# A graph network on one core: a shorter last edge batch, zeros for the padding rows from a tile of their own, and the last count store on another queue

## The chip, the core and the metric

The kernel runs on one core of a Trainium2 chip. The core has TensorE for matrix products (PE in the profile, PEld for its weight loads), VectorE (DVE), ScalarE (ACT), GpSimd (POOL) and SyncE (SP). Here SP does nothing but issue DMAs. ScalarE issues some too: a DMA that stands in ScalarE's order is issued when its turn comes, between its other instructions. TensorE writes its results to PSUM, and VectorE and ScalarE carry them from there to SBUF.

The metric is the device time of one execution in microseconds (us). The kernel before took 1538.35 us, the median of 3 runs from 1538.09 to 1540.38. The profile comes from one further execution.

## The reference, cut to what matters

There are 3125 nodes with 128 features and 103125 edges, sorted by their destination: 50000 random pairs in both directions and one loop per node. Four graph layers follow each other, each added to its input and normalised. The first multiplies by a weight matrix and sums over the edges with a weight per edge; the second is graph attention with four heads, the third attention between neighbours, the fourth two rounds of averaging over neighbours.

```python
# layer 0
xw = x @ weight
out = relu(segment_sum(edge_val[:, None] * xw[edge_col], edge_row) + b)
x = layernorm(x + out)
# layers 1 to 3 need for each pair (destination, source) only how many edges join them
```

## The kernel before, in words

The kernel turns the edge list into two dense matrices over 25 x 25 blocks of 128 nodes (`NB` = 25, so 3200 rows and columns for 3125 nodes; the last 75 are padding). One, `wd`, holds for each pair of nodes the sum of the edge weights in f32. The other, `f_ctd`, holds the count of edges in bf16, transposed. Both go to HBM. Layer 0 multiplies with `wd`; the layers after it read `f_ctd`.

**The start (lines 558 to 753).** The edges are loaded, keys are computed and stored as the table `td`, and five indirect DMAs on GpSimd (line 646) gather the edges of 128 groups of nodes each. `keys_of` turns one gather into keys in bf16 (copies on ScalarE and VectorE, lines 532, 534, 667, 687, 691, transposes on TensorE). ScalarE's queue carries the small loads: weights, biases, `f_att` (lines 538, 700, 711). The rows of `x` come over SP; the last 53 of them are a DMA of their own (line 642), after which SP issues nothing until the first store of the loop.

**The edge loop (lines 811 to 901).** A group is 5 nodes (`WN`), a batch 16 groups (`BW`), so there are 40 batches of 80 nodes (`NBT` = 40), the last for nodes 3120 to 3199. For each batch, `make` has VectorE compare the keys with a ramp to get one-hot matrices: `ohd` and `ohc` (line 824, two instructions of 128 x 4096) and `wod`, `ohd` scaled by three parts of the weight (line 833, three instructions). ScalarE scales 16 more columns of 128 for the third part (line 842, in `more`, four at a time). `make(b + 1)` is called before batch `b` is multiplied, so VectorE works one batch ahead. TensorE then does four groups of four windows: 8 matmuls into `cp` (counts, line 864) and 24 into `wp` (weights, line 872). ScalarE copies `cp` into `cs` (line 877) and `wp` into `ws` (line 883). After each batch SP stores `ws` to `wd` in two DMAs (line 885: 112 and 13 partitions, runs of 512 B), and after every second batch `cs` to `f_ctd` (line 888: 3200 runs of 320 B).

As soon as a block row of `wd` (128 nodes) is stored, `add0` loads it in two halves, `cw` (line 790, three buffers of 640 KB), and multiplies it with `xw` for 20 of the 25 column blocks (line 794). Block row 23 needs batches up to 38, block row 24 needs batches 38 and 39. The last block rows are done after the loop (line 900). Then come `bias0` for the five other column blocks (line 782), the normalisation of layer 0 (`end0`, line 799), and a second pass over `wd` for those five blocks (line 1162).

**What sets the order.** The program is written in the tile framework: a scheduler puts every engine's instructions in one order and adds the waits, and each engine and each queue keeps that order. The DMAs of SP's and ScalarE's queues get eight completion semaphores in turn, in the order of the program; a DMA is issued only when the last user of its semaphore has landed. Buffers come from pools; a tile waits until the work on the buffer's last tile is over.

Of the kernel before, what the change touches and what calls it, by code (L numbers as in the profile page):

```python
# [7 lines left out]
F32 = mybir.dt.float32  # L8
# [3 lines left out]
OP = mybir.AluOpType  # L12
# [3 lines left out]
P = 128  # L16
N = 3125
NB = 25
NP = NB * P
# [470 lines left out]
WN = 5  # L490
NW = 640
NG = 5
BW = 16
KW = WN * NB
NBT = NW // BW
Z0 = 20
V1 = 100
GA = 80.0
# [7 lines left out]
def fast_path(  # L506
# [4 lines left out]
    nc = tc.nc  # L511
# [3 lines left out]
    ctd = dram.tile([NB, P, NP], BF16, name="f_ctd")  # L515
    wd = dram.tile([NP, NP], F32, name="wd")
# [49 lines left out]
    ep = front.enter_context(tc.tile_pool(name="f_ep", bufs=1))  # L566
    cps = front.enter_context(tc.tile_pool(name="f_cps", bufs=3, space=PSUM))
    ramp = ep.tile([P, P], BF16, name="ramp")
# [156 lines left out]
    def products_of_weights():  # L725
        nc.gpsimd.tensor_tensor(both, gb_row, sb_row, OP.add)
        tw = {}
        for name, w in (("l1", l1_wt), ("q", wqt), ("k", wkt), ("v", wvt)):
            t = zps.tile([P, P], F32, name="trw", tag="acc3")
            nc.tensor.transpose(t, w, ident)  # L730
            tw[name] = ep.tile([P, P], F32, name="tw_" + name)
            nc.scalar.copy(tw[name], t)
        t = zps.tile([P, P], F32, name="trw", tag="acc3")
        nc.tensor.matmul(t[:, 0 : 2 * H], tw["l1"], att, start=True, stop=True)
        nc.scalar.copy(watt, t[:, 0 : 2 * H])
        t = zps.tile([P, P], F32, name="trw", tag="acc3")
        nc.tensor.matmul(t, tw["q"], tw["k"], start=True, stop=True)
        nc.scalar.copy(wyv[:, 0:P], t)
        t = zps.tile([P, P], F32, name="trw", tag="acc3")
        nc.tensor.matmul(t, tw["v"], wot, start=True, stop=True)  # L740
        nc.scalar.copy(wyv[:, P:], t)

    def xw_of(b0, n):

        t = zps.tile([P, 512], F32, name="trx", tag="acc0")
        for k in range(n):
            nc.tensor.transpose(t[:, k * P : (k + 1) * P], x[:, b0 + k, :], ident)
        xT = ep.tile([P, 512], F32, name="f_xTb", bufs=2)
        nc.scalar.copy(xT[:, : n * P], t[:, : n * P])
        t = zps.tile([P, 512], F32, name="trx", tag="acc2")  # L750
        for k in range(n):
            nc.tensor.matmul(t[:, k * P : (k + 1) * P], xT[:, k * P : (k + 1) * P], l0_wt, start=True, stop=True)
        nc.scalar.copy(xw[:, b0 : b0 + n, :].rearrange("p b d -> p (b d)"), t[:, : n * P])
# [26 lines left out]
    def bias0(acc, n):  # L780
        for j in range(n):
            nc.tensor.matmul(acc[:, j, :], ones, l0_br, start=(j == 0), stop=False, skip_group_check=True)
# [16 lines left out]
    def end0(acc, b0, n):  # L799
        t = lp0.tile([P, 4, P], F32, name="r0")  # L800
        nc.vector.scalar_tensor_tensor(
            t[:, 0:n, :], acc[:, 0:n, :], 0.0, x[:, b0 : b0 + n, :], OP.max, OP.add
        )
        layer_norm(lp0, x[:, b0 : b0 + n, :], t, (0, n), True)
# [3 lines left out]
    SB = 2  # L808
    wv_ = wd.rearrange("(w i) (c d) -> w (i c) d", i=WN, d=P)

    def make(b):

        if b % 8 == 2 and 8 < b < NBT - 8:
            keys[b // 8 + 1] = keys_of(b // 8 + 1)
        kd2, kc2, w2, w3 = keys[b // 8]
        ohd = op_.tile([P, 2 * BW, P], BF16, name="ohd")
        ohc = op_.tile([P, 2 * BW, P], BF16, name="ohc")

        def twos(k):
            k = k[:, b % 8, :, :, :].rearrange("p q w t -> p (q w) t")  # L820
            return k[:, :, None, :].to_broadcast([P, 2 * BW, P // 2, 2])

        for o, k in ((ohd, kd2), (ohc, kc2)):
            nc.vector.tensor_tensor(
                o.rearrange("p w (a t) -> p w a t", t=2), twos(k),
                ramp.rearrange("p (a t) -> p a t", t=2)[:, None, :, :].to_broadcast([P, 2 * BW, P // 2, 2]),
                OP.is_equal,
            )
        wod = []
        for s in range(3):  # L830
            f = of_.tile([P, 2 * BW, P], BF16, name="wod")
            n = 2 * BW if s < 2 else BW
            nc.vector.tensor_tensor(  # L833
                f[:, 0:n].rearrange("p w (a t) -> p w a t", t=2), ohd[:, 0:n].rearrange("p w (a t) -> p w a t", t=2),
                twos(w2[s])[:, 0:n], OP.mult,
            )
            wod.append(f)

        def more(k):
            for w in range(k, k + 4):  # L840
                at = (b % 8) * BW + w
                nc.scalar.activation(wod[2][:, BW + w, :], ohd[:, BW + w, :], AF.Copy, scale=w3[:, 1, at : at + 1])  # L842

        return ohd, ohc, wod, more

    cs = None
    acc0 = None
    done = 0
    cur = make(0)
    for k in range(0, BW, 4):  # L850
        cur[3](k)
    for b in range(NBT):
        ohd, ohc, wod, _ = cur
        cur = make(b + 1) if b + 1 < NBT else None
        if b % SB == 0:
            cs = sp.tile([P, NB, SB * BW * WN], BF16, name="cs")
        ws = sp.tile([P, BW, P], F32, name="ws")
        for k in range(0, BW, 4):
            cp = cps.tile([P, 4, P], F32, name="cp", tag="cw")
            wp = cps.tile([P, 4, P], F32, name="wp", tag="cw")  # L860
            for j in range(4):
                for q in range(2):
                    w = q * BW + k + j
                    nc.tensor.matmul(  # L864
                        cp[:, j, 0:KW], ohd[:, w, :], ohc[:, w, 0:KW], start=(j == 0 and q == 0), stop=(j == 3 and q == 1),
                        skip_group_check=True,
                    )
            for j in range(4):
                for q in range(2):
                    w = q * BW + k + j  # L870
                    for s in range(3):
                        nc.tensor.matmul(  # L872
                            wp[:, j, :], ohc[:, w, :], wod[s][:, w, :], start=(j == 0 and q == 0 and s == 0),
                            stop=(j == 3 and q == 1 and s == 2), skip_group_check=True,
                        )
            i0 = (b % SB) * BW * WN + k * WN
            nc.scalar.copy(  # L877
                cs[:, :, i0 : i0 + 4 * WN].rearrange("p c (w i) -> p c w i", i=WN),
                cp[:, :, 0:KW].rearrange("p w (i c) -> p c w i", c=NB),
            )  # L880
            if cur:
                cur[3](k)
            nc.scalar.copy(ws[:, k : k + 4, :], wp)  # L883
        for a, e in ((0, 112), (112, KW)):
            nc.sync.dma_start(wv_[b * BW : (b + 1) * BW, a:e, :].rearrange("w k d -> k w d"), ws[a:e, :, :])
        if b % SB == SB - 1:
            i0 = (b - SB + 1) * BW * WN
            nc.sync.dma_start(ctd[:, :, i0 : i0 + SB * BW * WN].rearrange("c d i -> d c i"), cs)
        if b < 2:
            for blocks in GB[4 * b : 4 * b + 4]:  # L890
                xw_of(*blocks)
        if b == 2:
            products_of_weights()
            acc0 = [zps.tile([P, 4, P], F32, name=f"acc{k}", tag=f"acc{k}") for k in range(Z0 // 4)]
            for a in acc0:
                bias0(a, 4)
        while acc0 and (done + 1) * P <= (b - 1) * BW * WN:
            add0(zp, done, acc0, (0, Z0))
            done += 1
    for i in range(done, NB):  # L900
        add0(zp, i, acc0, (0, Z0))
    front.close()
# [147 lines left out]
    with ExitStack() as st:  # L1050
# [20 lines left out]
        zpp = zero.enter_context(tc.tile_pool(name="f_zpp", bufs=1, space=PSUM))  # L1071
        left = GB[Z0 // 4 :]
        acc1 = [zpp.tile([P, 4, P], F32, name=f"left{k}") for k in range(len(left))]
        t8 = zpp.tile([P, 512], F32, name="tr_sa")
        for a, (b0, n) in zip(acc1, left):
            bias0(a, n)
        for g in range(Z0 // 4):
            end0(acc0[g], *GB[g])
# [73 lines left out]
        def top():  # L1152
            heads(0, Z0)
            ex = fp.tile([P, H], F32, name="ex", bufs=1)
# [135 lines left out]
        for x_, (g, hp, c) in enumerate(items):  # L1290
            i0, n = IG[g]
# [42 lines left out]
    with ExitStack() as st:  # L1334
# [79 lines left out]
        for x_, (q, c) in enumerate(items):  # L1414
            i0, n = QG[q]
# [5 lines left out]
            if q == 0 and NB - 4 <= c < NB - 1:  # L1421
                a = split + (c - NB + 4) * 512
# [6 lines left out]
            elif c == NB - 1:  # L1429
# [5 lines left out]
                for k0 in range(0, n, 3):  # L1435
                    m = min(3, n - k0)
                    t = acc[k0 // 3][:, 0 : m * (P + 1)].rearrange("p (b d) -> p b d", d=P + 1)
# [3 lines left out]
                    for j in range(m):  # L1441
                        b = i0 + k0 + j
# [9 lines left out]
    with ExitStack() as st:  # L1452
# [8 lines left out]
        for g in range(3, len(GB)):  # L1461
            b0, n = GB[g]
# [18 lines left out]
        for b in range(NB - HB):  # L1481
# [5 lines left out]
            if b == 18:  # L1487
# [3 lines left out]
                t = ps.tile([P, 512], F32, name="tr")  # L1491
# [37 lines left out]
        for k in range(K + 3):  # L1529
            if k < K:  # L1530
                for b in range(NB - HB, NB):
                    add1(last[b], b, k)
                c, n = CH[k]
# [86 lines left out]
```

## Time and profile before

| | before |
|---|---|
| median of 3 runs | 1538.35 us |
| the profiled execution | 1536.56 us |
| its span | 1534.5 us |
| TensorE busy | 1400.5 us (91%) |
| VectorE, ScalarE busy | 981.0, 923.4 us |
| mean granted TensorE clock | 0.979 |
| first one-hot matrix starts (line 824) | 31.45 us |
| last matmul of the edge loop starts a run of 1.50 us (line 872) | 467.27 us |
| matmuls of block rows 23 and 24 (line 794) | 487.28 to 497.87 us |
| DMA packets, bytes | 210368, 224.39 MB |

Times in the profile count from the start of the span. In the timeline a row is a run of equal instructions: start, duration, engine, line, operation, output and inputs, number; in brackets how long the engine was idle before it and what ended that. SPq and ACTq are DMA issues on the two queues; their duration is the time from the first issue of the row to the end of the last, waits within the row included. In the windows a row is a stretch of time, with the busy time of each engine (and its instructions), the granted TensorE clock as a share, the mean busy share of the 16 DMA engines, and what they moved in GB/s. The durations are those of one execution.

### The profile page before, as it was taken

The page shows a single profiled execution, that of the slowest core. Times are in us where ns is not written, and L with a number is a line of the kernel's source. Part 1 is how long each engine was busy: PE and PEld are TensorE (multiplying, and loading weights), DVE is VectorE, ACT ScalarE, POOL GpSimd, SP SyncE. Part 2 cuts the span into 40 slices and gives each one's busy share as a digit, 9 for nine tenths or more (in the row PEclk, how much of TensorE's full clock was granted, in tenths as well). Part 3 has the DMA queues.
Part 4 walks back from the last instruction along what each step waited for, and adds up shares of the span by engine and source line. Part 5 has one row for each costly group of instructions (what it writes and reads, how often), then busy time and mean ns, then how long its engine had stood idle before and what let it go on. Part 6 is the DMA issues. An engine that isn't in the chain of part 4 may idle for free.

```text
span 1534.5 us, 35155 instructions
## 1 busy us (share of the span) xinstructions
PE 1400.5 (91%) x14871; PEld 1223.6 (80%) x14871; DVE 981.0 (64%) x1574; ACT 923.4 (60%) x1880; POOL 122.5 (8%) x136
## 2 busy tenths in 40 slices
PE   4899999999997978899989989899999989999995
PEld 3898999998997867899979889577777764458995
DVE  4999899989991389778878887544464360012005
ACT  2988778888882489878778676544474340023006
POOL 1000000000000023203311320300000000000000
PEclk9999999999999999999999999999999999999998
DMA  6387787878877623444434333332222226513551
GB/s 192 91 220 207 203 234 206 235 202 223 214 214 232 222 85 101 143 118 125 132 115 134 114 87 95 106 94 68 67 72 73 82 105 238 193 44 129 195 195 45
DMA packets 210368, 224.39 MB, mean 146 GB/s; under 512 B 72892, under 2 KB 184007, under 8 KB 209945
## 3 DMA queue, kind: packets, MB, share of 16 engines
q1 hardware_dynamic: 206344, 217.74, 48.4%
q10 hardware_dynamic: 3457, 2.35, 0.6%
q8 instruction: 118, 1.93, 0.5%
q0 software_dynamic: 400, 1.97, 0.4%
q14 instruction: 49, 0.40, 0.1%
HBM read 157.67 MB, written 64.36 MB: 145 GB/s over the span
## 4 chain that ended last, share of the span: by engine, by line
PE 40%; DVE 5%; ACT 2%; issue 1%; POOL 1%; DMA 1%; DVEq 0%; ACTq 0%; SPq 0%; POOLq 0%
PE acc L1381 9%; PE s L1373 8%; PE acc L1476 7%; PE acc L1549 6%; PE acc L1241 4%; PE acc L1236 2%; DVE cm L1226 1%; DVE nz L1260 1%; PE tr L1513 1%; PE acc L1513 1%; DMA ct<-f_ctd 1%; ACT fm L1225 1%; DVE cm L1219 0%; PE tr L1505 0%; PE acc L1505 0%
## 5 line engine op out<-in xcount | busy, mean ns | idle before, releaser
L1241 PE MATMUL acc<-vp,cm 128*128 128x198 bf16 x2500 | 344.7, 252 | 6.6 <-DVE cm L1226 4.1
L1225 ACT ACTIVATE fm<-adr,bas 128x896 bf16<-128x896 f32 (+1 forms) x320 | 286.5, 952 | 68.0 <-DVE cm L1226 63.1
L1236 PE MATMUL acc<-vp,ct 128*128 128x204 bf16 x1250 | 315.2, 256 | 10.0 <-DVE vp L1144 5.6
L1241 PEld LDWEIGHTS <-cm 128*128 128x128 bf16 x2500 | 236.0, 98 | 26.5 <-issue 10.6
L872 PE MATMUL wp<-wod,ohc 128*128 128x128 bf16 x3840 | 244.0, 219 | 8.8 <-ACT cs L877 6.6
L872 PEld LDWEIGHTS <-ohc 128*128 128x128 bf16 x3840 | 224.0, 98 | 9.8 <-issue 9.4
L833 DVE TENSOR_TENSOR wod<-ohd,w 128x4096 bf16<-128x4096 bf16 (+1 forms) x120 | 225.0, 1931 | 0.6 <-PE wp L872 0.6
L1226 DVE TENSOR_TENSOR cm<-fm,ct 128x896 bf16<-128x896 bf16 (+1 forms) x320 | 198.1, 649 | 36.1 <-PE acc L1241 14.1
L842 ACT ACTIVATE wod<-ohd,wu 128x128 bf16<-128x128 bf16 x640 | 197.0, 400 | 0.0
L1377 DVE TENSOR_TENSOR e<-e,ct 128x416 f32<-128x416 f32 (+1 forms) x175 | 110.4, 636 | 108.2 <-ACT e L1376 102.6
L1376 ACT ACTIVATE e<-s,f_nm 128x416 f32<-128x416 f32 (+1 forms) x175 | 111.5, 642 | 99.4 <-PE s L1373 94.1
L1381 PEld LDWEIGHTS acc<-self__8127,e 128*128 128x128 f32 x1250 | 148.4, 193 | 21.5 <-issue 19.7
L1373 PE MATMUL s<-yT,f_xT 128*128 128x416 f32 (+1 forms) x350 | 145.8, 552 | 4.6 <-ACT rt L1356 4.0
L1381 PE MATMUL acc<-self__8127,e 128*128 128x129 f32 x1250 | 148.7, 276 | 0.6 <-DVE e L1377 0.6
L794 PE MATMUL acc<-f_xw,cw 128*128 128x128 f32 x1000 | 118.4, 278 | 7.4 <-DMA cw<-wd 7.4
L1236 PEld LDWEIGHTS <-ct 128*128 128x128 bf16 x1250 | 122.4, 98 | 2.5 <-issue 1.5
L883 ACT COPY ws<-wp 128x512 f32<-128x512 f32 x160 | 93.6, 585 | 49.8 <-PE wp L872 48.2
L794 PEld LDWEIGHTS acc<-f_xw,cw 128*128 128x128 f32 x1000 | 115.0, 194 | 7.6 <-DMA cw<-wd 7.6
L864 PE MATMUL cp<-ohc,ohd 128*128 128x125 bf16 x1280 | 96.7, 218 | 21.1 <-ACT ws L883 17.9
L1373 PEld LDWEIGHTS s<-yT,f_xT 128*128 128x128 f32 x350 | 62.2, 191 | 57.7 <-issue 40.6
L1476 PE MATMUL acc<-ct,ip 128*128 128x512 bf16 (+1 forms) x525 | 104.9, 360 | 1.4 <-DMA ct<-f_ctd 1.4
L1549 PE MATMUL acc<-ip,ct 128*128 128x128 bf16 x1875 | 105.2, 219 | 0.0
(277 smaller groups left out, 1482.7 us busy)
## 6 DMA issues: line engine op xcount, KB each, us to landing
ct<-f_ctd SPq DMA_DIRECT2D x50, 800.0 KB
wd<-ws SPq DMA_DIRECT2D x40, 896.0 KB
ct<-f_ctd SPq DMA_DIRECT2D x150, 224.0 KB
cw<-wd SPq DMA_DIRECT2D x50, 640.0 KB
f_ctd<-cs SPq DMA_DIRECT2D x20, 1000.0 KB
ct<-f_ctd SPq DMA_DIRECT2D x25, 416.0 KB
ct<-f_ctd SPq DMA_DIRECT2D x25, 384.0 KB
cw<-wd SPq DMA_DIRECT2D x25, 320.0 KB
```

The source lines that it names most:

```text
L794: nc.tensor.matmul(accs[j // 4][:, j % 4, :], cw[:, j - h, :], xw[:, i, :], start=False, stop=(i == NB - 1 and (j % 4 == 3 or j == n - 1)) ...
L833: nc.vector.tensor_tensor(f[:, 0:n].rearrange("p w (a t) -> p w a t", t=2), ohd[:, 0:n].rearrange("p w (a t) -> p w a t", t=2), twos(w2[s] ...
L842: nc.scalar.activation(wod[2][:, BW + w, :], ohd[:, BW + w, :], AF.Copy, scale=w3[:, 1, at : at + 1])
L872: nc.tensor.matmul(wp[:, j, :], ohc[:, w, :], wod[s][:, w, :], start=(j == 0 and q == 0 and s == 0), stop=(j == 3 and q == 1 and s == 2), ...
L1225: nc.scalar.activation(f[:, : n * P], at, AF.Relu, bias=bas[:, c, h : h + 1], scale=UP)
L1226: nc.vector.tensor_tensor(m[:, : n * P], f[:, : n * P], ct[:, : n * P], OP.min)
L1236: nc.tensor.matmul(out_(F1, PW), ct[:, k * P : (k + 1) * P], vp[:, c, hp : hp + 2, :, 2 * F1 : V1], start=(c == 0), stop=False, skip_group ...
L1241: nc.tensor.matmul(out_(0, 2 * F1)[:, j], ms[j][:, k * P : (k + 1) * P], vp[:, c, hp + j, :, 0 : 2 * F1], start=False, stop=(c == NB - 1 a ...
L1373: nc.tensor.matmul(s[:, :m], xT[:, c * P : (c + 1) * P], yT[:, i0 * P + a : i0 * P + a + m], start=True, stop=True)
L1381: nc.tensor.matmul(acc[k // 3][:, (k % 3) * (P + 1) : (k % 3 + 1) * (P + 1)], es[q, c][:, k * P : (k + 1) * P], vo[:, c, 0 : P + 1], start ...
L1476: nc.tensor.matmul(acc[k][:, :n], ips[b // 4][:, b % 4, s, :], ct[:, c : c + n], start=(b == 0 and s == 0), stop=(b == NB - 1 and s == 2),)
L1549: nc.tensor.matmul(acc[g][:, j, :], ct[:, (b0 + j) * P : (b0 + j + 1) * P], ups[b // 4][:, b % 4, s, :], start=(b == 0 and s == 0 and j == ...
```

## The change

The last batch, number 39, covers nodes 3120 to 3199, of which only 3120 to 3124 exist. The change computes four of its 16 groups (`LW` = 4), nodes 3120 to 3139, which is one of TensorE's four groups of four windows. VectorE's instructions for it are cut to these columns, two slices where there was one whole. The rest of its counts in `cs` is set to zero on GpSimd. The rows of `wd` for nodes 3140 to 3199 are stored from a tile of zeros, `none`, by four DMAs of 15 rows; each is 128 x 15 runs of 25 floats (100 B). They are written in the code behind batch 1; in the order of the changed program they stand on SP directly behind the load of the last 53 rows of `x`. The store of `cs` after the last batch is issued by ScalarE instead of SP; in ScalarE's order it stands behind the last `cs` copy and before the last `ws` copy. Apart from the last two batches, and these DMAs, the order of the instructions on each engine is the same as before.

```diff
+LW = 4
@@ fast_path
+    NL = (NBT - 1) * BW + LW
+    none = ep.tile([P, 15 * NB], F32, name="none")
+    nc.gpsimd.memset(none, 0.0)
@@ make(b)
+        def some(s):
+            if b < NBT - 1:
+                return [slice(0, 2 * BW if s < 2 else BW)]
+            return [slice(0, LW)] + ([slice(BW, BW + LW)] if s < 2 else [])
+
+        def packed(o, ww):
+            return o[:, ww].rearrange("p w (a t) -> p w a t", t=2)
+
         for o, k in ((ohd, kd2), (ohc, kc2)):
-            nc.vector.tensor_tensor(
-                o.rearrange("p w (a t) -> p w a t", t=2), twos(k),
...
+            for ww in some(0):
+                nc.vector.tensor_tensor(
+                    packed(o, ww), twos(k)[:, ww],
...
             f = of_.tile([P, 2 * BW, P], BF16, name="wod")
...
+            for ww in some(s):
+                nc.vector.tensor_tensor(packed(f, ww), packed(ohd, ww), twos(w2[s])[:, ww], OP.mult)
@@ the loop over batches
+        nw = BW if b < NBT - 1 else LW
         if b % SB == 0:
             cs = sp.tile([P, NB, SB * BW * WN], BF16, name="cs")
+            if b + SB == NBT:
+                nc.gpsimd.memset(cs[:, :, ((SB - 1) * BW + LW) * WN :], 0.0)
-        for k in range(0, BW, 4):
+        for k in range(0, nw, 4):
...
-            if cur:
+            if cur and (b + 1 < NBT - 1 or k < LW):
                 cur[3](k)
...
-            nc.sync.dma_start(wv_[b * BW : (b + 1) * BW, a:e, :].rearrange("w k d -> k w d"), ws[a:e, :, :])
+            nc.sync.dma_start(wv_[b * BW : b * BW + nw, a:e, :].rearrange("w k d -> k w d"), ws[a:e, 0:nw, :])
+        if b == 1:
+            for i in range(NL * WN, NP, 15):
+                nc.sync.dma_start(
+                    wd[i : i + 15, :].rearrange("i (p k) -> p i k", p=P), none.rearrange("p (i k) -> p i k", k=NB)
+                )
         if b % SB == SB - 1:
             i0 = (b - SB + 1) * BW * WN
-            nc.sync.dma_start(ctd[:, :, i0 : i0 + SB * BW * WN].rearrange("c d i -> d c i"), cs)
+            eng = nc.scalar if b == NBT - 1 else nc.sync
+            eng.dma_start(ctd[:, :, i0 : i0 + SB * BW * WN].rearrange("c d i -> d c i"), cs)
```

More of the change, by code (lines that the diff above doesn't have):

```diff
@@ L821, in twos @@
             return k[:, :, None, :].to_broadcast([P, 2 * BW, P // 2, 2])
-        for o, k in ((ohd, kd2), (ohc, kc2)):
-            nc.vector.tensor_tensor(
-                o.rearrange("p w (a t) -> p w a t", t=2), twos(k),
-                ramp.rearrange("p (a t) -> p a t", t=2)[:, None, :, :].to_broadcast([P, 2 * BW, P // 2, 2]),
-                OP.is_equal,
-            )
+        def some(s):
[4 more added lines that the diff above has]
+            return o[:, ww].rearrange("p w (a t) -> p w a t", t=2)
+        for o, k in ((ohd, kd2), (ohc, kc2)):
+            for ww in some(0):
+                nc.vector.tensor_tensor(
+                    packed(o, ww), twos(k)[:, ww],
+                    ramp.rearrange("p (a t) -> p a t", t=2)[:, None, :, :].to_broadcast(
+                        [P, ww.stop - ww.start, P // 2, 2]
+                    ),
+                    OP.is_equal,
+                )
         wod = []
@@ L831, in make @@
             f = of_.tile([P, 2 * BW, P], BF16, name="wod")
[L832 to L836, printed above, removed]
+            for ww in some(s):
+                nc.vector.tensor_tensor(packed(f, ww), packed(ohd, ww), twos(w2[s])[:, ww], OP.mult)
             wod.append(f)
@@ L884, in fast_path @@
         for a, e in ((0, 112), (112, KW)):
-            nc.sync.dma_start(wv_[b * BW : (b + 1) * BW, a:e, :].rearrange("w k d -> k w d"), ws[a:e, :, :])
+            nc.sync.dma_start(wv_[b * BW : b * BW + nw, a:e, :].rearrange("w k d -> k w d"), ws[a:e, 0:nw, :])
[3 more added lines that the diff above has]
+                    wd[i : i + 15, :].rearrange("i (p k) -> p i k", p=P), none.rearrange("p (i k) -> p i k", k=NB)
+                )
         if b % SB == SB - 1:
             i0 = (b - SB + 1) * BW * WN
-            nc.sync.dma_start(ctd[:, :, i0 : i0 + SB * BW * WN].rearrange("c d i -> d c i"), cs)
+            eng = nc.scalar if b == NBT - 1 else nc.sync
+            eng.dma_start(ctd[:, :, i0 : i0 + SB * BW * WN].rearrange("c d i -> d c i"), cs)
         if b < 2:
```

## The prediction

> **What bounds the kernel now.** I read the page first. TensorE is busy 91% of the span, but the chain that ended last can be followed back only to 788 us, so it does not reach the edge loop (31 to 469 us) that the change edits. I therefore went through that loop and its seams in the timeline, then by windows, with the starts and sizes of the DMA packets in the trace. The end of the loop:
>
> ```profile
> 463.21 2.59 SPq L885 DMA_DIRECT2D wd<-ws  x2
> ...
> 465.89 7.54 SPq L790 DMA_DIRECT2D cw<-wd  x2
> ...
> 467.27 1.50 PE L872 MATMUL wp<-wod,ohc 128*128 128x128 bf16 x24
> ...
> 468.81 0.59 ACT L883 COPY ws<-wp 128x512 f32<-128x512 f32 x1 [0.71 <-PE wp L872]
> ...
> 469.45 1.38 PE L782 MATMUL left<-l_br,ones 128*128 128x128 f32 x10 [0.68 <-ACT ws L883]
> ...
> 470.66 9.25 PE L794 MATMUL acc<-f_xw,cw 128*128 128x128 f32 x80
> ...
> 473.52 3.22 SPq L885 DMA_DIRECT2D wd<-ws  x2
> ...
> 476.80 1.30 SPq L888 DMA_DIRECT2D f_ctd<-cs  x1
> ...
> 478.21 21.91 SPq L790 DMA_DIRECT2D cw<-wd  x9
> ...
> 487.28 10.59 PE L794 MATMUL acc<-f_xw,cw 128*128 128x128 f32 x80 [7.37 <-DMA cw<-wd]
> ```
>
> The columns are start, duration, engine or queue. Batch 39 runs on TensorE from 461.1 to 468.8. Meanwhile SP waits to issue the second half of block row 22's load: the three `cw` buffers are full until block row 21's first half is multiplied (472.97). So batch 39's store, ready at 469.4, is issued at 473.52, the count store behind it at 476.80, and the loads of block rows 23 and 24 only from 478.21. TensorE sits idle 7.37 us until 487.28.
>
> ```profile
> core 0: us, PE busy (x) PEld busy (x) DVE busy (x) ACT busy (x) POOL busy (x), PEclk, DMA share, GB/s
> ...
> 462.00:474.00 12.00, 11.18 (x156) 10.89 (x154) 0.09 (x2) 6.62 (x13) 1.45 (x2) 1.00 0.84 264
> 474.00:480.00 6.00, 5.91 (x52) 5.64 (x50) 0.00 (x0) 0.00 (x0) 0.00 (x0) 1.00 1.04 285
> 480.00:487.00 7.00, 0.00 (x0) 0.00 (x0) 0.06 (x1) 0.00 (x0) 0.00 (x0) 0.74 1.09 278
> 487.00:498.00 11.00, 10.59 (x80) 10.40 (x80) 3.63 (x21) 0.54 (x2) 0.00 (x0) 0.85 0.42 154
> ```
>
> From 474 to 487 the DMA engines are full (share over 1), and from 480 TensorE has nothing: the packets show batch 39's 2000 of 512 B until 479.5, then 3200 counts of 320 B until 484.5, then the loads. The stall makes TensorE's clock fall to half from 483.4 to 490.2; 80 matmuls take 10.59 us after it, 9.25 before it. This seam is a DMA bound with TensorE behind it.
>
> The start of the kernel:
>
> ```profile
> 22.96 1.20 POOL L646 DMA_INDIRECT eg<-td,row_i  x1 [12.28 <-DMA f_att<-in_L_gnn_att_dst_dram]
> ...
> 23.46 0.44 ACTq L538 DMA_DIRECT2D f_w1l<-in_L_gnn_w_l_dram  x1
> ...
> 24.43 0.45 ACTq L538 DMA_DIRECT2D f_b<-in_L_gnn_b_dram  x1
> ...
> 27.39 0.41 ACT L667 COPY wei<-eg 128x256 f32<-128x256 f32 x1 [13.74 <-DMA f_b<-in_L_gnn_b_dram]
> ...
> 27.40 0.39 ACTq L538 DMA_DIRECT2D f_w2l<-in_L_gnn_w_l_dram  x1
> ...
> 28.35 0.48 ACTq L538 DMA_DIRECT2D f_b<-in_L_gnn_b_dram  x1
> ...
> 28.87 0.59 ACT L749 COPY f_xTb<-trx 128x512 f32<-128x512 f32 x1 [1.07 <-issue]
> ...
> 31.45 2.28 DVE L824 TENSOR_TENSOR ohd<-kd,ramp 128x4096 bf16<-128x4096 bf16 x1
> ```
>
> ScalarE issues weight loads in the middle of its work. The copies that give the first keys begin only after the load of `b2` is issued (28.35 + 0.48), and run without a gap until VectorE can start `ohd` at 31.45. From there VectorE has no idle time (79.83 of 80 us from 60 to 140); later it and TensorE wait for each other (278.28 and 278.47 of 300 us from 140 to 440), but for nothing from outside the loop, so a delay before 31.45 moves everything. From 35 to 54 us the DMA engines do nearly nothing after the gathers.
>
> **What the Trainium skill says.** (1) DMA: Bandwidth & Descriptors, Specifications: line rate wants at least 512 B, below it the engine does read-modify-write. The trace agrees that small is dear: median 27 ns per 512 B, 21 ns per 320 B, 9 ns per 4 B. It has no 100 B write. (2) The same page, Queues, rings and completion order: SP's and ScalarE's queues are rings on the same 16 engines; each ring keeps its order, and an engine takes turns between rings. (3) The same page, Why a DMA increments its semaphore by 16 and not by 1: the number of engines must divide the slowest dimension, so a transfer over 53 partitions uses one engine. The trace agrees: the 53 rows of `x` trickle from 20.6 to 22.9 at 24 packets per us. (4) TensorE: Matmul & The Clock Gate, Part 1: idle windows of some 3.4 us halve the clock; here the drop came 3.5 us into the stall.
>
> **The change, part by part.**
>
> *Fewer groups in batch 39.* Three of four groups go: 3 x (8 + 24) matmuls, at 1.78 us a group (starts at 453.82, 455.60, 457.38): 5.3 us of TensorE on the path. Its end moves from 468.8 to about 463.4. VectorE makes a quarter of the one-hot tiles in nine instructions instead of five (10.2 to about 3 us), and ScalarE drops 12 scalings of 0.3 us and six copies of 0.58 us. VectorE's part is worth nothing by itself: it already waits in this seam until 494.34. Batch 38 stays bound by TensorE (1.78 us pace).
>
> *Smaller store, count store on the other queue.* 1500 packets of 512 B go: 1500 x 27 ns / 16 = 2.5 us of all engines. The count store keeps its 3200 packets (4.2 us) but is issued by ScalarE after its last `cs` copy, near 462.4, 14 us earlier; its issue (0.4 us when a ring is empty, as at 62.70, up to 1.7) stands before the last `ws` copy, and TensorE's bias matmuls wait for that copy. That costs up to 1.5 us of TensorE, covered because block row 21's load lands only at 466.1 at the earliest. The new store now shares the engines with the loads of rows 21 and 22 and makes those late, so TensorE cannot use its 5.3 us directly; what counts is the queue of DMA work up to row 23. Before, 462 to 486.4: 19.4 us of packets (five loads at 1.57, stores 3.4 + 3.4, counts 4.2, a rest of 0.5), 1.5 us idle (472.4 to 474), so the other 22.9 us ran at 0.85. After: 2.5 / 0.85 = 3.0 us less work, and no idle 1.5 us, because the queue is never dry: row 23 lands 4.5 us sooner, near 482.7. TensorE then works through rows 22 to 24 without a 7 us hole, so I take the 1.35 us of half clock as saved, less 0.3 us of small waits: 5.6 us. Bounds: 3.5 (half clock falls elsewhere, mixing two rings costs efficiency) to 8 (packets run at 1.0). TensorE's 5.3 us is not added; the DMA queue has swallowed it.
>
> *Zero stores.* Four DMAs of 1920 packets of 100 B. In the order of the changed program they stand on SP right after the 53 rows of `x`, far ahead of batch 1, and their zero tile is ready by 3 us. The first can issue at 19.5, the second when the edge table's half has landed (21.7), the third at 22.9, the fourth at 23. SP has nothing else until 53.95. Both queues hand out eight completion semaphores in turn, and a DMA waits until its semaphore's last user has landed. Four more DMAs shift the turns: on ScalarE the last `f_att` load now waits for zero store 1, `w1l` for store 2, `w2l` for store 3. Behind `w2l` stand `w2r`, `b2`, and all the copies above. On the slowest engine the zeros queue behind the rows of `x` until 22.9; each store is 120 packets there. At 14 ns (9 plus a third of the way to 320 B's 21 by size gives 13, and one for unaligned rows) three stores take 5.0 us, 1.3 us of gathers come between, 0.4 us to land: 29.6. `w2l` was issued at 27.40: 2.2 us late, and so is `ohd`. Bounds: 0 (9 ns, or the zeros pass while the engines are empty) to 5 us (21 ns); worse with read-modify-write. The gathers themselves may land 1 us later, under the same delay.
>
> *The rest.* The two memsets on GpSimd have idle time around them (it waits 437 us before 468.88). The weight loads of the start have their users far later.
>
> Sum: -5.6 + 2.2 = -3.4 us. The profiled execution was 1536.56 us, of which 1534.5 span and 2.06 around it; it becomes 1533.2 (span 1531.1). The median of the runs shown, 1538.35, is 1.8 above the profiled one; the forecast against it is 1535.0.
>
> **Rivals.**
>
> A: the zeros cost nothing. They fit in the thin DMA time from 20.5 to 25 (share 0.05 to 0.5), land before `w2l` is due, and the seam pays 5 to 8 us: about 1532. For it: little else moves then. Against it: the single engine that carries the 53 rows.
>
> B: the seam gives little. The early count store delays rows 21 and 22, cold clock returns in the holes between them, and the gain is 3 us or less, eaten by the start: 1537.5 to 1539. For it: nearly all bytes stay. Against it: the idle 1.5 us and 1500 packets do leave.
>
> C, slower: zero packets of 100 B are dearer than any in this trace. The place is `w2l` behind zero store 3. With a price of p ns the delay is 22.9 + 3 x 0.12p + 1.7 - 27.4 us: it eats the 5.6 us at p = 23 ns, and is measurably slower (8.7 us) at p = 32; at 36 it gives 1543. For it: writes under 512 B that also cut memory lines appear nowhere before. Against: 320 B writes stay at 21.
>
> **How the numbers follow.** Changes within 0.2% (3.1 us) are about what a measurement here cannot tell from none. Forecast 0.58: 1532 to 1538 by its own bounds; its centre lies just beyond 3.1 us, so 0.36 of it falls on faster and 0.22 on same. A 0.19, all but 0.01 faster. B 0.11, all same. C 0.12: 0.10 slower, 0.02 between. Together 0.54, 0.36, 0.10. The range leaves out a tenth at each end: 1529.8 (A with 8 us and more) to 1540.8 (C's beginning).
>
> **What would show it.** Right: the first `ohd` starts at 33 to 34 us, ScalarE's `w2l` issue near 29.6, no gap over 5 us before the last 80 `cw` matmuls, which end, measured from the first `ohd`, about 5.6 us earlier than the 466.4 us of before; the loop between unchanged. Wrong: `ohd` still at 31.4 (A), beyond 36 (C), or row 23 landing no earlier relative to it (B). An effect in the later stages, from 545 us on, which should only shift, would make all of this wrong: so would half-clock windows of 3.4 us falling differently there.

## The result and the profile after

The kernel became slower. The changed kernel takes 1546.52 us (median of 9 runs, 1541.86 to 1547.90) against 1538.09 us for the kernel before (9 runs, 1535.87 to 1540.38), a ratio of 1.0050 with a 95% interval of 1.0039 to 1.0062, or 6.0 to 9.5 us. The forecast was 1535.0, its range ended at 1540.8. In the profiled executions the span grew by 10.0 us, from 1534.5 to 1544.5, and it splits at three marks: the first `ohd`, the `ohd` of batch 39, and the end of the last matmul of block row 24.

| us | before | changed | difference |
|---|---|---|---|
| start of the span to the first `ohd` | 31.45 | 46.71 | +15.26 |
| first `ohd` to that of batch 39 | 419.30 | 420.16 | +0.87 |
| from there to the end of block row 24 (the seam) | 47.13 | 41.89 | -5.24 |
| from there to the end of the span | 1036.58 | 1035.74 | -0.84 |

So the seam paid almost what was forecast and the start lost seven times what was forecast. This is the start in the timeline of the changed kernel, with its columns as before (start, duration, engine or queue, line, operation, tiles, number; in brackets the idle time before and what ended it):

```profile
19.66 13.98 SPq L904 DMA_DIRECT2D wd<-none  x4
...
22.73 9.15 ACTq L712 DMA_DIRECT2D f_att<-in_L_gnn_att_dst_dram  x4
...
33.34 0.35 ACTq L539 DMA_DIRECT2D f_w1l<-in_L_gnn_w_l_dram  x1
...
34.16 0.35 DVE L660 TENSOR_SCALAR kic<-eg,thr 128x256 f32<-128x256 f32 x1 [15.65 <-DMA eg<-td,row_i]
...
35.22 0.40 ACT L668 COPY wei<-eg 128x256 f32<-128x256 f32 x1 [20.66 <-issue]
...
42.55 0.39 ACTq L539 DMA_DIRECT2D f_w2l<-in_L_gnn_w_l_dram  x1
...
44.15 0.58 ACT L750 COPY f_xTb<-trx 128x512 f32<-128x512 f32 x1 [8.53 <-issue]
...
46.71 2.28 DVE L838 TENSOR_TENSOR ohd<-kd,ramp 128x4096 bf16<-128x4096 bf16 x1
```

Two things are late. The first gather has landed at 34.1 us (before: 27.4), seen in `kic`, its first reader. And ScalarE, done with `wei` at 35.62, does nothing until it issues `w2l` at 42.55. The profile calls that idle time "issue": it shows nothing there that the engine waits for. The landings name it: the third zero store lands at 42.5 us, and it is the last user of the semaphore whose turn `w2l` has. From `w2l` to `ohd` it takes 4.16 us (before: 4.05). Meanwhile the DMA engines are not idle. In the windows (stretch, busy time of the engines, granted TensorE clock, DMA share, GB/s):

```profile
core 0: us, PE busy (x) PEld busy (x) DVE busy (x) ACT busy (x) POOL busy (x), PEclk, DMA share, GB/s
...
28.00:34.00 6.00, 0.00 (x0) 0.00 (x0) 0.00 (x0) 0.00 (x0) 0.00 (x0) 0.50 1.10 127
```

Not one engine computes, the DMA share is 1.10, and 127 GB/s move. In the seam of the kernel before the same share moved 278 to 285 GB/s. The seam of the changed kernel, in the timeline and in windows:

```profile
478.40 0.40 ACTq L910 DMA_DIRECT2D f_ctd<-cs  x1
...
485.78 9.58 SPq L901 DMA_DIRECT2D wd<-ws  x2
...
491.45 6.22 PE L795 MATMUL acc<-f_xw,cw 128*128 128x128 f32 x40 [4.51 <-DMA cw<-wd]
495.46 15.54 SPq L791 DMA_DIRECT2D cw<-wd  x9
...
499.56 9.20 PE L795 MATMUL acc<-f_xw,cw 128*128 128x128 f32 x80 [1.89 <-DMA cw<-wd]
```

```profile
480.00:491.00 11.00, 5.79 (x50) 5.41 (x48) 0.00 (x0) 0.92 (x1) 0.56 (x1) 1.00 1.06 331
491.00:497.00 6.00, 5.55 (x36) 5.56 (x37) 0.00 (x0) 0.00 (x0) 0.00 (x0) 0.72 0.68 182
```

The hole of 7.37 us before the last 80 matmuls has become holes of 4.51 and 1.89 us. Measured from the `ohd` of batch 39, those 80 start 3.85 us sooner, and at full clock they take 9.20 us instead of 10.59. The half clock still came, but it fell on the 40 matmuls at 491.45 (6.22 us instead of 4.73), whose successors waited for a load anyway.

One wait in this seam is a turn of the semaphores again. SyncE's row at 485.78 holds batch 39's two stores to `wd`, and the second was issued only at 495.04. The last user of its semaphore was the count store, now on ScalarE's queue, which landed at 495.02. In the window from 494 to 496 us the DMA engines have a share of 0.09 and move 20 GB/s. So the idle stretch ahead of block row 23, which the prediction counted as saved (1.5 us before), came back.

### The profile page after: what moved, and what is told of

It reads as the page before. It is cut to its first block, busy times and chain, and to the rows that moved or that the text cites. A ratio compares the mean times of both kernels' runs of the same rounds, so it can differ in the third digit from the quotient of the medians.

```text
span 1544.5 us, 34966 instructions
## 1 busy us (share of the span) xinstructions
PE 1397.0 (90%) x14775; PEld 1219.6 (79%) x14775; DVE 975.3 (63%) x1578; ACT 916.6 (59%) x1862; POOL 125.1 (8%) x138
## 3 DMA queue, kind: packets, MB, share of 16 engines
HBM read 157.67 MB, written 64.36 MB: 144 GB/s over the span
## 5 line engine op out<-in xcount | busy, mean ns | idle before, releaser
L888 PE MATMUL wp<-wod,ohc 128*128 128x128 bf16 x3768 | 239.1, 219 | 7.1 <-ACT cs L893 6.6
L888 PEld LDWEIGHTS <-ohc 128*128 128x128 bf16 x3768 | 219.8, 98 | 8.4 <-issue 8.2
L849 DVE TENSOR_TENSOR wod<-ohd,w 128x4096 bf16<-128x4096 bf16 (+2 forms) x122 | 221.1, 1868 | 0.6 <-PE wp L888 0.6
L855 ACT ACTIVATE wod<-ohd,wu 128x128 bf16<-128x128 bf16 x628 | 193.1, 400 | 0.0
```

Source lines behind the costliest of these rows:

```text
L849: nc.vector.tensor_tensor(packed(f, ww), packed(ohd, ww), twos(w2[s])[:, ww], OP.mult)
L888: nc.tensor.matmul(wp[:, j, :], ohc[:, w, :], wod[s][:, w, :], start=(j == 0 and q == 0 and s == 0), stop=(j == 3 and q == 1 and s == 2), ...
```

## The experiments

Three questions: is the start all of the loss, what makes four zero stores so dear, and which part of the change gives the gain at the seam? The theory: 7680 writes of 100 B hold up everything that shares the memory with them, and through the turn of the semaphores they hold up ScalarE too. Its rivals: the turn alone; the scattered addresses; the mere number of small writes. The zeros also had to be measured with little beside them. In the table, the seam is the third row of the table above; the ratio is to runs of the kernel before on the same chip.

| kernel | first `ohd` | seam | span | median us | ratio (95%) |
|---|---|---|---|---|---|
| changed | 46.71 | 41.89 | 1544.5 | 1546.52 | 1.0050 (1.0039 to 1.0062) |
| zeros_only | 41.09 | 48.77 | 1543.6 | 1547.79 | 1.0080 (1.0066 to 1.0095) |
| zeros_in_one_place | 47.42 | 41.46 | 1542.4 | 1545.61 | 1.0060 (1.0046 to 1.0075) |
| weights_on_sp | 34.21 | 43.09 | 1535.8 | 1537.40 | 1.0003 (0.9994 to 1.0012) |
| big_runs | 33.66 | 42.26 | 1529.1 | 1530.18 | 0.9955 (0.9942 to 0.9968) |
| early_128 | 33.35 | 43.59 | 1530.1 | 1531.72 | 0.9971 (0.9958 to 0.9983) |
| late_zeros | 31.85 | 42.26 | 1527.8 | 1530.16 | 0.9953 (0.9939 to 0.9967) |
| runs_and_late | 30.91 | 42.16 | 1526.9 | 1529.04 | 0.9957 (0.9944 to 0.9970) |
| runs_and_sp | 32.34 | 41.73 | 1529.9 | 1531.44 | 0.9967 (0.9954 to 0.9980) |
| count_store_on_act | 30.63 | 46.95 | 1533.0 | 1535.30 | 0.9991 (0.9983 to 1.0000) |

late_128, late_500 and changed_again (the changed kernel once more) have one execution each, from which both the profile and the time come: 1531.09, 1529.72 and 1542.10 us, beside 1537.68 for one of the kernel before. The first three columns come from one profiled execution per kernel.

### The zeros in 512 long runs (big_runs)

```diff
-    wd[i : i + 15, :].rearrange("i (p k) -> p i k", p=P), none.rearrange("p (i k) -> p i k", k=NB)
+    wd[i : i + 15, :].rearrange("i c -> (i c)").rearrange("(p k) -> p k", p=P), none
```

> The kernel after, with the same zeros stored by four DMAs of 128 runs of 1500 B (512 packets in all) instead of 7680 of 100 B. ScalarE's load of `w2l` still waits for a zero store (now the fourth). Theory 'packets' (the many small writes hold up the reads and themselves): first `ohd` at 31.5 to 33 us instead of 46.7, the gathers land as before (first 27 to 28 us), total 1531 to 1534 us. Rival 'turn' (four more DMAs in the turn of completion semaphores, whatever their size): `ohd` stays beyond 40 us, total above 1541. Rival 'elsewhere' (the loss does not hang on the start): `ohd` comes early, the total stays above 1541.

Timeline of this variant:

```profile
29.62 0.39 ACTq L539 DMA_DIRECT2D f_w2l<-in_L_gnn_w_l_dram  x1
...
33.66 2.28 DVE L838 TENSOR_TENSOR ohd<-kd,ramp 128x4096 bf16<-128x4096 bf16 x1
```

The same bytes in the same place, with a zero store still in the turn ahead of `w2l`, and `ohd` starts 13.05 us sooner than in the changed kernel: 0.66 us beyond the upper end expected, the first gather at 29.6 us against 27 to 28. The total is 0.8 us under the lower end. "Turn" and "elsewhere" fall; what was dear is how the zeros are cut into packets.

### The same packets, but after the gathers (late_zeros)

```diff
-    nc.gpsimd.memset(none, 0.0)
+    nc.gpsimd.tensor_scalar(none, egs[4].rearrange("p a t k -> p (a t k)")[:, 0 : 15 * NB], 0.0, None, OP.mult)
```

> The kernel after, with the zero tile computed on GpSimd from the fifth gathered block (times 0), so that the same 7680 packets of 100 B can only start when the gathers are over, in the stretch of 35 to 54 us in which the DMA engines do nearly nothing. Theory 'packets beside reads': `ohd` at 31 to 32 us, the zeros then take 7 to 12 us and hide, total 1531 to 1534 us. Rival 'dear by themselves': alone on the engines they still take 17 us and more, land after 54 us and hold batch 0's store; total 1535 and above.

Timeline and, below it, windows of this variant:

```profile
31.85 2.28 DVE L838 TENSOR_TENSOR ohd<-kd,ramp 128x4096 bf16<-128x4096 bf16 x1
...
38.33 8.08 SPq L904 DMA_DIRECT2D wd<-none  x4
```

```profile
39.00:41.00 2.00, 1.18 (x10) 0.94 (x10) 2.00 (x2) 1.98 (x6) 0.00 (x0) 1.00 0.78 98
...
43.00:49.00 6.00, 5.45 (x98) 5.40 (x97) 6.00 (x4) 6.00 (x18) 0.00 (x0) 1.00 1.67 46
```

The start is whole again, as the first theory said; the total is 0.8 us under its lower end. But the zeros took 15.7 us (39.3 to 55.0) with hardly another packet beside them, longer than the 7 to 12 expected, and the last of their completions came at 58.4 us: 19.1 us, as the rival "dear by themselves" had it. They still held up next to nothing: batch 0's store is issued 22.7 us after the first `ohd`, before the change 22.5. The windows show a fast phase and a slow one: 98 GB/s at first, later 46 GB/s at a DMA share of 1.67. In the packet records the first 2,300 or so, up to 41.3 us, go at 1160 per us and take 13 ns each, close to the 14 of the prediction. The others go at 390 per us: that is 41 ns of one engine for each, on 16 engines. Over the whole, 480 packets per engine in 15.7 us are 33 ns each. So 13 ns holds for a burst; behind it stands a slower drain.

### Nothing on ScalarE waits for the zeros (weights_on_sp)

```diff
-    nc.scalar.dma_start(t, ap)
+    late = name in ("f_wo", "f_w1l", "f_w1r", "f_b1", "f_w2l", "f_w2r", "f_b2")
+    (nc.sync if late else nc.scalar).dma_start(t, ap)
```

> The kernel after, with ScalarE's seven loads from `wo` to `b2` issued by SyncE ahead of the zero stores, so that nothing on ScalarE waits for a zero store; the zeros still run beside the gathers. Theory: of the 15.3 us at the start 8.5 are ScalarE's wait for the third zero store and the rest comes from gathers that land 7 us late; `ohd` at 37 to 40 us, total 1537 to 1541 us. Rival 'semaphore alone': `ohd` at 31 to 33 us, total near 1532. Rival 'gathers alone': `ohd` stays at 45 to 47, total near 1546.

`ohd` came at 34.21, earlier than theory expected; the total is inside its range, but for another reason. The seven loads now stand ahead of the zeros on SyncE, so the first zero packet starts at 26.6 instead of 21.8 us and the first gather escapes most of it (28.4 us, before 27.4). The second lands at 32.9 (before 28.9), and copies of its edges stand ahead of `ohd` in the order of ScalarE and VectorE. The split was not the clean one intended. And the loop from first to last `ohd` took 424.1 us instead of 419.3: the scheduler also put stores and loads of the first batches in another order on SyncE, which was not followed further. What it does show: with the zeros behind the first gather and no wait on them, 7680 small packets cost the start 2.8 us, not 15.

### The 100 B packets side by side (zeros_in_one_place)

```diff
-    none = ep.tile([P, 15 * NB], F32, name="none")
+    none = ep.tile([P, 15, NB + 1], F32, name="none")
...
-    wd[i : i + 15, :].rearrange("i (p k) -> p i k", p=P), none.rearrange("p (i k) -> p i k", k=NB)
+    wd[i : i + 15, :].rearrange("i c -> (i c)").rearrange("(p j k) -> p j k", p=P, k=NB), none[:, :, 0:NB]
```

> The kernel after, with the same 7680 packets of 100 B, but the 15 that a partition writes follow each other in memory (1500 B in one piece) instead of lying 12.8 KB apart. Theory 'number of small writes': no change, zeros land by 42 to 46 us, `ohd` 45 to 48, total 1544 to 1548. Rival 'scattered addresses': writes into neighbouring bytes are cheap, `ohd` at 33 us or earlier, total near 1533.

The spare column keeps the 15 runs of a partition apart in SBUF, and the trace has 7680 packets of 100 B as before. `ohd` is at 47.42 and the last zero packet at 48.1 us (2 us later than expected), as with scattered addresses. That rival falls.

### Only the zeros, batch 39 whole (zeros_only)

```diff
+    if b == 1:
+        for i in range(NL * WN, NP, 15):
+            nc.sync.dma_start(wd[i : i + 15, :]..., none...)
```

> The kernel before with only the four stores of 100 B zeros added at the start (batch 39 stays whole and writes its rows once more at the end). Theory (the start carries the whole loss, the seam's gain is not in it): first `ohd` at 46 to 48 us, total 14 to 16 us above the kernel before, 1550.5 to 1553. Rival (part of the 10 us in the span of the changed kernel comes from elsewhere): less than 12 us above, under 1549.

By time it is 12.2 us slower, between the two expectations; that is 3.8 us more than the changed kernel's 8.4, which is the seam's gain within the intervals. Its profiled execution, the fastest of the four, lost only 9.6 us at the start:

```profile
35.76 0.35 DVE L659 TENSOR_SCALAR kic<-eg,thr 128x256 f32<-128x256 f32 x1 [18.82 <-DMA eg<-td,row_i]
...
36.52 0.39 ACTq L538 DMA_DIRECT2D f_w2l<-in_L_gnn_w_l_dram  x1
...
41.09 2.28 DVE L828 TENSOR_TENSOR ohd<-kd,ramp 128x4096 bf16<-128x4096 bf16 x1
```

Here the third zero store landed at 36.5, just behind the first gather, so that the late gather accounts for most of the delay and the wait for the semaphore adds little. In all four profiles with early 100 B zeros and the loads on ScalarE, `w2l` is issued within 0.05 us of that landing: 36.5, 42.1, 42.5 and 43.4 us. The third store is issued when the 53 rows of `x` have landed: at 22.9 here, as before the change, and at 24.3 to 25.3 in the other three. That those 1.4 to 2.3 us make the 5.5 to 6.9 us at `w2l` is not shown. The seam is 1.6 us longer than before because 10.2 us of half clock (6.8 before) came with the last hole: the last 80 matmuls took 12.06 us instead of 10.59.

### The changed kernel again (changed_again)

> The changed kernel once more, to see how far the delay at its start differs between executions: the start of the kernel before with the same zero stores began `ohd` at 41.1 us, the changed one at 46.7, that with the zeros in one place at 47.4. Theory 'spread of the executions': `ohd` anywhere from 40 to 48 us, and span minus `ohd` near 1497.8 as in the first profile. Rival 'fixed': 46.5 to 47.0 again, then the kernel with whole batch 39 differs for a cause of its own.

`ohd` at 46.56, `w2l` at 42.07; 1542.10 us. That is the rival's value: two executions of the changed kernel agree within 0.2 us. That speaks for a cause of its own in zeros_only, but of that kernel there is one profile only, so chance isn't ruled out. Its rows of `x` came sooner; why is open. Span minus `ohd` is 1493.5 us and not 1497.8: the 0.87 us in the loop did not return (419.30), and the rest came after the seam (see "The later stages" below).

### Small packets on and off the multiples of 128 B (late_128, late_500, early_128)

```diff
+    zs = wd[NL * WN : NP, :].rearrange("i c -> (i c)").rearrange("(m p j k) -> m p j k", m=5, p=80, k=32)
+    for m in range(5):
+        nc.sync.dma_start(zs[m], none[:80, :, 0:32])
```

For packets of 500 B the same with m=4, p=128, k=125 and a tile to match.

> The variant with late zeros, storing the same bytes in 6000 packets of 128 B that each begin at a multiple of 128 B (five stores), in the quiet stretch after the gathers. The 7680 packets of 100 B took 15.7 us there: 1207 per us at first, 300 to 500 per us from the 2,700th on. Theory 'a small write costs as such': again about 450 per us, 12 to 14 us in all. Rival 'pieces of a memory line': a write that covers whole aligned pieces has no such price, 1000 per us and more to the end, 5 to 7 us in all.

> The variant with late zeros, storing the same bytes in 1536 packets of 500 B (four stores), unaligned, in the quiet stretch. Theory 'a price per small write, here some 2.2 ns of the whole memory path': 1536 packets in 3 to 4 us. Rival 'below 512 B a write is dear by its bytes' (the 45 GB/s of the 100 B stores): 768 KB in 15 us and more.

Windows of the variant with 128 B:

```profile
41.00:43.00 2.00, 1.82 (x21) 1.52 (x18) 2.00 (x2) 2.00 (x8) 0.00 (x0) 1.00 0.75 122
43.00:47.00 4.00, 3.31 (x60) 3.31 (x60) 4.00 (x3) 4.00 (x12) 0.00 (x0) 1.00 0.61 97
```

There is no slow phase: the DMA share stays at 0.6 to 0.75 where the 100 B packets had 1.67. From the packet records, all in the same quiet stretch:

| packets | from first to last, us | ns of one, first 2 us | ns of one, 4 to 6 us in |
|---|---|---|---|
| 7680 of 100 B | 15.7 | 13 | 52 (43 to 45 us) |
| 6000 of 128 B, each at a multiple of 128 B | 6.1 | 13 | 13 |
| 1536 of 500 B, not at multiples | 6.0 | 28 | 72 (43 to 45 us) |
| 512 of 1500 B, not at multiples | 3.2 | 67 | (over) |

The times are means. 6000 aligned packets take 6.1 us, so the number of small writes is not the cause; 500 B packets slow down as the 100 B ones do, from about the 1,000th on, and took 6.0 us where one theory said 3 to 4 and the other 15. The 1500 B packets did not slow down, but there are only 512 of them, fewer than either of the others sent before its slow phase.

The kernel before holds one more case: the last count store, 3200 packets of 320 B, goes from 479.5 to 485.1 us at 20 to 28 ns each (means by the microsecond), up to 830 per us, without a slow phase. Its packets begin at multiples of 64 B in `f_ctd`, and each covers two and a half pieces of 128 B. So if cut pieces are the cause, the pieces are not 128 B but 64 B or less.

The Trainium skill (DMA: Bandwidth & Descriptors, Specifications) says that below 512 B the engine does read-modify-write. The slow phases at 100 and 500 B would fit that; 128 B and 320 B, also below 512 B, have none. That the slow phase is this read-modify-write is an inference. The profile doesn't show it: the bytes read from HBM are 157.67 MB in the kernel before and in every variant, so either nothing more is read or that count leaves it out. That it matters where a packet begins, and not only how long it is, is argued too: no run stored 128 B packets off the multiples. The same 128 B packets beside the gathers:

> The changed kernel with its zeros stored early as there, but as 6000 packets of 128 B that begin at multiples of 128 B (five stores of 1200). In the order of its program one load on ScalarE's queue (`f_att`) waits for a zero store, the first. Theory 'cut pieces': 6000 small packets beside the rows of `x` and the gathers harm little, because they cut nothing: zeros over by 29 us, first gather landed by 30 us, `ohd` at 32 to 35 us, total 1530 to 1534. Rival 'many small writes beside reads': as with 100 B the gathers slow down, the first lands after 33 us, zeros over beyond 35 us, `ohd` beyond 38, total above 1537.

```profile
19.66 6.72 SPq L905 DMA_DIRECT2D wd<-none  x5
...
33.35 2.29 DVE L838 TENSOR_TENSOR ohd<-kd,ramp 128x4096 bf16<-128x4096 bf16 x1
```

`ohd` is at 33.35, the first gather landed at 28.8, the total is inside the range of "cut pieces". The zeros were over only at 33.3 us, not 29, though all were issued by 26.4: from 27 us on they share the engines with the gathers, at 302 to 708 packets per us. That harmed little. In this order of the program fewer of ScalarE's loads wait for zeros, so the 13.4 us between this and the changed kernel hold both effects. The first gather, which is issued without waiting for a zero store, carries 5.3 us of it by itself (34.1 to 28.8).

### The queue of the last count store (runs_and_sp, count_store_on_act)

```diff
-    eng = nc.scalar if b == NBT - 1 else nc.sync
+    eng = nc.sync
```

> The variant with zeros in runs of 1500 B, with the last count store back on SyncE's queue, where it is issued after batch 39's stores. Theory: of the 5.2 us at the seam some 1.5 come from the DMA queue that no longer runs dry because this store starts early; 1531.5 to 1532.5 us against 1530.2. Rival 'fewer groups alone': no difference, 1529.7 to 1530.7. Rival 'queue alone': the seam's gain is gone, 1535 and above.

Timelines at the seam, first with SyncE's queue, then with ScalarE's (big_runs):

```profile
470.28 0.89 SPq L901 DMA_DIRECT2D wd<-ws  x2
...
471.22 0.38 SPq L908 DMA_DIRECT2D f_ctd<-cs  x1
...
483.02 10.82 PE L795 MATMUL acc<-f_xw,cw 128*128 128x128 f32 x80 [3.91 <-DMA cw<-wd]
```

```profile
464.50 0.40 ACTq L908 DMA_DIRECT2D f_ctd<-cs  x1
...
472.75 8.92 SPq L901 DMA_DIRECT2D wd<-ws  x2
...
486.02 9.20 PE L795 MATMUL acc<-f_xw,cw 128*128 128x128 f32 x80 [1.63 <-DMA cw<-wd]
```

Measured from the `ohd` of batch 39 (452.11 and 452.96), block row 23 is there 2.15 us sooner with SyncE's queue. There batch 39's two stores go out within 0.89 us; with ScalarE's queue the second is issued at 481.35, when the count store has landed (481.33), and from 480 to 482 us the DMA share is 0.08. With SyncE's queue it is 0.97 or more from 460 to 483, in nine windows of 1 to 5 us. What this gains is lost at TensorE, which waited 3.91 us in one piece, fell to half clock, and takes 10.82 us for the last 80 instead of 9.20. The seam is 41.73 against 42.26 us: no gain from the move. The 1531.44 us lie between the two expectations, 0.06 under the theory's; the two ratios overlap, and the 0.8 us by which the span is longer come after the seam (+2.2 us there).

> The kernel before with only the last count store moved to ScalarE's queue; batch 39 whole, no zero stores. Theory: 1.5 to 2 us of the seam's 5.2 us come with the early store, so 1534.5 to 1535.2 against 1536.6. Rival 'queue alone': 5 us, 1531.5. Rival 'it costs': its issue holds up the last `ws` copy and its 3200 packets delay the loads of block rows 21 and 22, 1536.6 to 1538.

The move alone makes the seam 46.95 us instead of 47.13. By the ratio the kernel gains 1.4 us, but the interval reaches to zero and the medians differ by 0.3 us (1535.57 before); in the profile 0.82 of 1.5 us lie at the start, which the edit doesn't touch. By the seams the theory that gave this store 1.5 us falls: the shorter batch alone gives the gain there. Which of its two parts gives it, the 1500 packets or the three groups of matmuls that go, no run separates.

### Both remedies (runs_and_late)

> Both remedies together: 512 zero packets of 1500 B, started only after the gathers, from 38 us. Theory: the start is that of the kernel before (`ohd` 31.3 to 31.9) and the zeros take 2 to 3 us in the quiet stretch; 1528 to 1530.2 us, not slower than either remedy alone (1530.2). Rival: what the two remedies leave is not at the start; no difference from 1530.2.

The zero tile of late_zeros with the runs of big_runs: `ohd` at 30.91, the zeros over in 3.2 us, 1529.04 us and a ratio of 0.9957 (0.9944 to 0.9970), no measurable difference to either remedy alone. It beats both kernels: 6.5 us under the kernel before, measured beside it; the changed kernel is 8.4 over it. One of the two remedies is enough.

## Why the prediction was wrong

**The step that failed: "Zero stores", +2.2 us; it measured +15.26.** The path was right to the instruction: four more DMAs shift the turns, `w2l` waits for zero store 3, and `ohd` follows. Its sizes were wrong, all in one direction, and a second path, the late gathers, which the step took as 1 us under the same delay, made about half of the loss:

- *14 ns a packet.* It was interpolated by size between 4 B and 320 B packets. Measured with little beside it (late_zeros), a 100 B packet costs 33 ns of an engine's time over the whole and 41 ns after the burst. The median there is still 13 ns, the mean 45; one who reads the median alone sees nothing.
- *"1.3 us of gathers come between" and the gathers "may land 1 us later".* The first gather landed 6.8 us later. The packets of the five gathers (6144 B) took 525 ns in the mean beside the zeros and 303 before.
- *Store 3 issued at 22.9.* The 53 rows of `x` landed at 25.29, so store 3 was issued at 25.30. Why they came later is open: beside the same store 1 they landed at 22.94 in zeros_only.

Together `w2l` came at 42.55 instead of 29.6. Rival C had put the place and the formula: 22.9 + 3 x 0.12p + 1.7. With the 33 ns of late_zeros it gives 36.5, and zeros_only shows 36.52. That agreement is luck in part: the formula allows 1.3 us for the gathers, and in zeros_only the first of them landed 8.4 us late. How the other 6 us of the changed kernel divide between the later issue and the gathers is not shown. C also named a possible reason, writes under 512 B that cut memory lines, and that none was in the trace. It was given a chance of 0.12 because 320 B writes "stay at 21"; but those lie on multiples of 64 B, so they say nothing on packets off them.

The two halves of the delay could not be separated by one clean edit. The trace of the changed kernel bounds them: ScalarE stood still 6.93 us (35.62 to 42.55) for nothing but the semaphore; the other 8.3 us of the 15.26 came before that, from a first gather 6.8 us late and ScalarE's earlier waits for zero stores 1 and 2.

**What held.** The seam: forecast -5.6, bounds 3.5 to 8, measured -5.24. Of its terms the row's load 3.85 us sooner (4.5 forecast) and the clock 1.39 (1.35 forecast). The gap before the last 80 matmuls is under 5 us, as said. One term of it failed, so that the fit of the sum is luck in part: the 1.5 us of idle DMA time was not saved, since the second store of batch 39 waited for the early count store. With that store on SyncE's queue the idle stretch is gone and the gain is as large, not larger, because the half clock returns. The loop is unchanged but for 0.87 us in one execution. Rival B, a poor seam, did not occur. Rival A, zeros that cost nothing, is what the change could have been: it gave 1532 against 1538.35, 6.4 us less, and late_zeros measures 6.5 us less.

**The later stages** should only shift, but their length differs too: 1036.58 us from the seam to the end before, 1032.3 to 1036.2 in the others. The steps are of one size. After the seam the clock records show 6.8 us of half clock in the kernel before, in the changed one, in runs_and_sp and count_store_on_act; 3.4 us in zeros_only, big_runs, early_128 and the late ones of the table; none in changed_again and late_500. Each 3.4 us less makes the block from there to the last `left` matmul 1.6 us shorter (-1.6 and -3.2 us against before). The Trainium skill (TensorE: Matmul & The Clock Gate, Part 1) has windows of that length that run free of the program; the prediction said such windows could fall differently there, and they did. So the last 1 to 3 us of a total are no evidence for an edit here.

## What to carry to other kernels

Before a store of many small pieces is put where "nothing happens", ask how long its pieces are and where they begin: the same 768 KB, stored beside the gathers, delayed the first `ohd` by 1 to 2 us in runs of 1500 B or in 128 B on multiples of 128, and by 10 to 16 us in runs of 100 B (3 us where the first gather was ahead of them). A price read from a median, or interpolated by size from packets of another kind, is the price of a burst; bound it by what the queue does when thousands of packets stand behind it. And where a framework deals out completion semaphores in turn, every added or moved DMA chooses which later DMA on another queue will wait for it, so look which instruction stands behind that one. It happened twice here: at the start with the zero stores, and in the seam with the count store.

## What was unexpected of the hardware

- The burst and the drain: with little beside them some 2,300 writes of 100 B go at 13 ns each, the others at 390 per us on all engines, about 39 to 46 GB/s (late_zeros). Reads beside such writes slow down: the gathers' 6144 B packets from a mean of 303 to 525 ns (changed kernel).
- Packets of 128 B that begin at multiples of 128 B kept about 1000 per us to the end of 6000 (late_128), and 3200 of 320 B at multiples of 64 B showed no slow phase either.
- 500 B off the multiples slows from 28 to 72 ns within 1536 packets; 1500 B does not in 512. Whether more of those would, and what decides it, the length, the place or the number, was not tried.
